# Where two operands of an edge kernel lie: targets' offsets and softmax marks read from PSUM

## The chip, the cores and the metric

The kernel runs on one core of one Trainium2 chip. The metric is the device time of one execution in microseconds; the time before is the median of three runs.

## The reference

A layer of a graph network with 12500 nodes of 128 channels and 400000 edges. The edges come sorted by target (`dst`). Cut to what matters:

```python
h = relu(layernorm(x))
message = (h @ w_src + b_src)[src] + (h @ w_dst)[dst]
rad_w = silu(silu(edge_attr_32 @ fc_w1 + fc_b1) @ fc_w2 + fc_b2) @ fc_w3 + fc_b3
message = message * edge_weight1 * rad_w
message = message @ w_sep + b_sep                    # 8 heads x (16 for scores + 16 values)
alpha = smooth_leaky_relu(message.heads[:, :, :16])
score = einsum("ehk,ahk->eh", alpha, alpha_dot)      # one score per edge and head
att = segment_softmax(score, dst)                    # over the edges of one target
out = segment_sum(value * att, dst) @ w_proj + b_proj
return x + out
```

## The kernel before, in words

**Tiling.** A first stage normalizes the nodes and writes two tables to DRAM, `t_src` and `t_dst` (one row of 128 per node). Then `windows` runs over the edges. A section is 512 edges (`SEC`), four tiles of 128; a step `k` works on two sections, 1024 edges, and there are 391 steps (`NP`). A last stage divides the sums, projects them and adds `x`. A second path, for edges that are not sorted, stands in an Else branch that does not run here.

**The order.** `tc.manual_schedule()` keeps the order in which the program is written, so each engine runs its instructions in the order in which `step` (L1053) calls the helpers. `step(k)` mixes work of several steps: it loads for steps up to `k + 6`, gathers for `k + 2`, does the small network of the edge attributes for `k + 3` to `k`, the message of `k`, the scores of `k - 1`, and the weighted values and sums of step `c = k - 13` (`LAG`), because the softmax of the edges lies between. Semaphores are set between engines wherever a tile is written by one and read by another.

**The gathers.** `gather(k, f)` (L819) issues, from POOL's queue, four indirect DMAs for a section, each of which fetches 128 rows of `t_src` by a column of `idx`, a tile in SBUF. There are three buffers for each of the two sections of a step. TensorE turns the fetched tiles in `sources` (L887, L892).

**Targets' offsets.** Every 16 steps `prep_load` loads sources and targets of 128 tiles as rows, `prep_make` (L746) subtracts from each target the first one of its section, and `prep_turn` (L755) turns both on TensorE, through one PSUM tile "misc", and copies them to SBUF: `idx` for the gathers and `loc` for `one_hot`. `one_hot(c)` (L987) compares `loc` with `lane` (0 to 127 in each partition) on VectorE (L991, 504 results per partition; L994, 8 more for the last place of the window). `sums(c)` (L1012, L1018) multiplies this with the weighted values and accumulates in "misc"; L1022 adds `bare` and leaves the result in `ob`.

**The softmax.** For eight steps (16 sections, 8 heads: 128 partitions of 512 scores) there is one round, `m`. `load_sm` (L942) loads marks from DRAM, one word for each edge that is 0 or a large negative number where a new target begins, with each section's row repeated for its 8 heads. `softmax_up` (L948, L950) and `softmax_down` (L953, L955) are two running maxima with these marks as the first operand; `softmax_exp` (L958) subtracts (L960) and takes Exp on ScalarE; `softmax_T` (L973) turns the result in four transposes through "misc" and copies it. They are called in steps 2, 3 and 4 of each eight, at the end of `step`.

**PSUM.** All eight banks are used: "m1", "misc", "p3" (two), "pa", "V", "pm0" and "pm1". "m1" serves `e_T`, `mlp1` and `scores`; "misc" serves `prep_turn`, `mlp1`, `softmax_T` and `sums`.

**Others that the prediction names.** `split_md` (L806) makes three bf16 parts of a tile in four pieces, two of them on VectorE (L813, L817). `values(c, f)` (L999) makes "V" on TensorE (L1005), and VectorE multiplies it by the weights into `pvx` (L1007). `alphas` (L909) and `alphas_sum` (L917, L919) make `al` from "pa". `radial` is L884, `message` L899 and L906. `add_x` (L1040, L1044) adds a bias to four node tiles in step 7 of each eight, 25 times in all.

Of the kernel before, what the change touches and what calls it, by code (L numbers as in the profile page):

```python
# [56 lines left out]
def gnn_kernel(ctx: ExitStack, tc: tile.TileContext, a: dict, out: bass.AP):  # L57
# [44 lines left out]
    def blocks(t0, t1):  # L102
# [17 lines left out]
                   allow_small_or_imprecise_dtypes=True)  # L120
    zc = 5
# [591 lines left out]
    def windows():  # L713
# [7 lines left out]
        with tc.tile_pool(name="wk2", bufs=2) as sp, tc.tile_pool(name="ps", bufs=1, space=PSUM) as pp, \  # L721
                tc.manual_schedule(), ExitStack() as held:
            lp = held.enter_context(tc.tile_pool(name="ld", bufs=2, side="right"))
            prep, e_g, d_g, w_g, md, gath = {}, {}, {}, {}, {}, {}
            eTs, h1s, h2s, ohT, m3, mr, mTs, als, S_all, sms, Ps, Pem, pvx, ohs, accs, xs, Ms, pms, p3s, rads, made = (
                {} for _ in range(21))
# [19 lines left out]
            def prep_make(u):  # L746
                ri, rb = made[u]
                rows = lp.tile([P, 2, P], F32, name="rows", bufs=1)
                rf = lp.tile([P, 1], F32, name="rf", bufs=1)
                nc.vector.tensor_copy(rf, rb)  # L750
                nc.vector.tensor_copy(rows[:T, 0, :], ri[:T, 0, :])
                nc.vector.tensor_scalar(rows[:, 1, 0:T], ri[:, 1, 0:T], rf, None, op0=ALU.subtract)
                made[u] = rows

            def prep_turn(u):  # L755
                rows = made.pop(u)
                pt = pp.tile([P, 2, P], F32, name="misc")
                nc.tensor.transpose(pt[:, 0, 0:T], rows[:T, 0, :], ident[:T, :T])
                nc.tensor.transpose(pt[:T, 1, :], rows[:, 1, 0:T], ident)
                if u:  # L760
                    idx = lp.tile([P, T], I32, name="idx")
                    nc.vector.tensor_copy(idx, pt[:, 0, 0:T])
                else:
                    idx = idx0
# [54 lines left out]
            def gather(k, f):  # L819
                gs = lp.tile([P, TS, C], F32, name=f"gs{f}", bufs=3)  # L820
                u = k // 16
                idx, _ = prep[u]
# [16 lines left out]
            def mlp1(k):  # L839

                p1 = [pp.tile([P, 2 * T], F32, name=n) for n in ("m1", "misc")]
# [100 lines left out]
            def load_sm(m):  # L942
                sms[m] = sp.tile([P, SEC + 1], BF16, name="sm")
                at = same[0:1, m * MQ * SEC:m * MQ * SEC + 1]
                at = bass.AP(at.tensor, at.offset, [[SEC, MQ], [0, H], [1, SEC + 1]])
                nc.sync.dma_start(out=sms[m], in_=at)

            def softmax_up(m):  # L948
                Ms[m] = sp.tile([P, 2, SEC], F32, name="M")
                nc.vector.tensor_tensor_scan(Ms[m][:, 0, :], sms[m][:, 0:SEC], S_all[m], RESTART,  # L950
# [491 lines left out]
```

## Time and profile before

| | us |
|---|---|
| median of 3 runs | 4320.27 |
| lowest, highest | 4319.8, 4326.04 |
| the profiled execution | 4318.65 |
| its span, first to last instruction | 4316.9 |

The mean granted TensorE clock in the profiled execution is 0.969. The first gather starts 89.2 us after the span's start and the last at 4113.6 us; what follows the last gather is the work of the last 13 steps, the joining of windows and the last stage.

How to read it: PE is TensorE's matmuls, PEld its loads of weights, DVE VectorE, ACT ScalarE, POOL GpSimd, SP the queue from which most DMAs are issued. L12 is line 12 of the kernel. A group's row has the line, engine and operation, the tiles out<-in, the shapes and the count, then the busy time and the mean of one in ns, then the engine's idle time just before and what ended it. A row of the timeline has the start, the duration, both in us, the engine, line and operation, and in brackets the idle time before it and what ended that. A row of windows has the stretch, its length, each engine's busy time with its count, the granted clock as a share, the share of the DMA engines and GB/s. A row of waits has who waited for whom, the total in us, how often and the longest.

### The profile page before, as it was taken

How to read it: one execution, taken by the hardware profiler on the slowest of the kernel's cores; microseconds unless marked ns; L12 is line 12 of the kernel's file. 1: busy time of each engine (PE TensorE's matmuls, PEld its weight loads, DVE VectorE, ACT ScalarE, POOL GpSimd, SP SyncE). 2: the span in 40 equal slices, each digit the busy share in tenths (PEclk: the TensorE clock that was granted, in tenths of full speed). 3: DMA queues.
4: the chain of work that ended last, by engine and by line, in shares of the span. 5: the costliest groups of instructions: out<-in, count | busy, mean ns of one | idle time of the engine just before them, and what ended most of it. 6: DMA issues, size and time to landing. Idle time of an engine off the chain costs nothing. (4 is left out here: it accounts for less than half of the span.)

```text
span 4316.9 us, 86772 instructions
## 1 busy us (share of the span) xinstructions
PE 3929.3 (91%) x29228; PEld 2402.1 (56%) x29228; DVE 3128.6 (72%) x6152; ACT 1919.4 (44%) x4505; POOL 3063.7 (71%) x3148
## 2 busy tenths in 40 slices
PE   6779999999999999999999999999999999999964
PEld 5335555555555555555555555555555555555553
DVE  6457777777777777777777777777777777777764
ACT  6334444444444444444444444444444444444411
POOL 1667777777777777777777777777777777777701
PEclk9889999999999999999999999999999999999987
DMA  5766776776776776776777776767676676676625
GB/s 192 236 191 177 195 191 178 197 189 174 195 190 171 198 189 177 192 191 183 187 188 190 182 185 179 178 186 183 171 187 184 175 187 182 171 187 178 164 60 191
DMA packets 592627, 788.16 MB, mean 183 GB/s; under 512 B 124473, under 2 KB 390814, under 8 KB 592044
## 3 DMA queue, kind: packets, MB, share of 16 engines
q1 hardware_dynamic: 384090, 519.34, 40.4%
q0 software_dynamic: 100416, 205.44, 23.1%
q10 hardware_dynamic: 107666, 57.76, 4.6%
q8 instruction: 232, 3.80, 0.4%
q14 instruction: 223, 1.83, 0.1%
HBM read 642.94 MB, written 139.58 MB: 181 GB/s over the span
## 5 line engine op out<-in xcount | busy, mean ns | idle before, releaser
L825 POOL DMA_INDIRECT gs<-t_src,idx x3125 | 3049.3, 976 | 1063.0 <-issue 783.0
L914 ACT ACTIVATE sl<-pa,c_b_a 128x512 f32<-128x512 f32 x782 | 536.9, 687 | 1123.6 <-PE pa L912 1108.2
L1005 PEld LDWEIGHTS V<-c_w_v,mT 128*128 128x128 f32 x6048 | 749.1, 195 | 315.8 <-DVE ob L1022 132.5
L1005 PE MATMUL V<-c_w_v,mT 128*128 128x128 f32 x6048 | 887.1, 291 | 0.0
L1007 DVE TENSOR_TENSOR pvx<-V,Pem 128x512 f32<-128x512 f32 x756 | 520.7, 689 | 476.7 <-PE V L1005 463.4
L912 PE MATMUL pa<-mT,c_w_a 128*128 128x512 f32 x1564 | 812.6, 602 | 8.0 <-DVE al L919 4.1
L919 DVE SCALAR_TENSOR_TENSOR al<-pa,sl 128x512 f32<-128x512 f32 x782 | 539.7, 690 | 361.1 <-ACT sl L914 356.1
L892 PEld LDWEIGHTS pm<-ident,gs 128*128 128x128 f32 x3125 | 397.7, 141 | 526.5 <-issue 406.8
L884 DVE SCALAR_TENSOR_TENSOR rad<-p,c_fc_b,w_b 128x512 f32<-128x512 f32 x782 | 549.9, 745 | 106.0 <-PE p L876 81.0
L1018 PEld LDWEIGHTS misc<-pvx,oh 128*64 128x64 f32 x6250 | 365.5, 141 | 414.8 <-ACT h L848 409.5
L1018 PE MATMUL misc<-pvx,oh 128*64 128x136 f32 x6250 | 469.3, 294 | 118.2 <-ACT h L848 118.2
L892 PE MATMUL pm<-ident,gs 128*128 128x128 f32 x3125 | 499.7, 277 | 77.7 <-DMA gs<-t_src,idx 73.2
L906 DVE SCALAR_TENSOR_TENSOR mT<-pm,c_b_src,rad 128x512 f32<-128x512 f32 x782 | 550.6, 746 | 25.4 <-PE pm L899 24.5
L862 ACT ACTIVATE h<-p,b 128x512 f32<-128x512 f32 x391 | 288.5, 738 | 435.3 <-PE p L859 369.3
L876 PE MATMUL p<-h,w3b 64*128 64x512 f32 x1564 | 409.4, 601 | 11.1 <-ACT h L862 11.1
L899 PE MATMUL pm<-ohT,m 64*128 64x512 bf16 x2346 | 321.2, 379 | 0.0
L932 ACT ACTIVATE Sp<-m,b_s 128x512 f32<-128x512 f32 x196 | 134.7, 687 | 418.4 <-PE m L929 416.3
L844 PE MATMUL m<-eT,w1b 64*128 64x256 f32 x782 | 276.0, 433 | 1.0 <-ACT eT L837 1.0
L844 PE MATMUL misc<-eT,w1b 64*128 64x256 f32 x782 | 276.0, 433 | 0.0
L859 PE MATMUL p<-h,w2b 64*64 64x256 f32 x3128 | 260.5, 403 | 13.7 <-DVE rad L884 13.7
L991 DVE TENSOR_TENSOR oh<-lane,loc 128x504 f32<-128x504 f32 x391 | 264.4, 676 | 0.0
L848 ACT ACTIVATE h<-misc,b 128x256 f32<-128x256 f32 x391 | 193.2, 494 | 138.4 <-PE misc L844 131.5
(165 smaller groups left out, 3626.3 us busy)
## 6 DMA issues: line engine op xcount, KB each, us to landing
w_b<-in_edge_weight SPq DMA_DIRECT2D x390, 512.0 KB
d_b<-in_dst SPq DMA_DIRECT2D x390, 256.0 KB
sc_d<-Sp SPq DMA_DIRECT2D x196, 256.0 KB
gs<-t_src,idx POOLq DMA_INDIRECT x3125
e_t<-in_edge_attr ACTq DMA_DIRECT2D x390, 128.0 KB
win<-ob SPq DMA_DIRECT2D x391, 68.0 KB
agg<-ob SPq DMA_DIRECT2D x782, 33.5 KB
md<-t_dst SPq DMA_DIRECT2D x782, 32.0 KB
```

The lines of the kernel that those rows point to most:

```text
L825: nc.gpsimd.indirect_dma_start(out=gs[:, t, :], out_offset=None, in_=t_src[:, :], in_offset=bass.IndirectOffsetOnAxis(ap=idx[:, t0 + t:t0 ...
L844: nc.tensor.matmul(p1[q], w1b[s, :], eTs[k][s, :], start=True, stop=True)
L876: nc.tensor.matmul(p3s[k][:, f, 0:SEC], w3b[s, :], h2s[k][s, :], start=True, stop=True)
L884: nc.vector.scalar_tensor_tensor(rad[:, s], p3[:, f, 0:n], b3, w_g[k][:, s], op0=ALU.add, op1=ALU.mult)
L892: nc.tensor.matmul(pms[k, f][:, t * T:(t + 1) * T], gs[:, t, :], ident, start=(t == 0), stop=False, is_transpose=True, skip_group_check=True)
L906: nc.vector.scalar_tensor_tensor(mTs[k][:, s], pms.pop((k, f))[:, 0:n], b_n, rad[:, s], op0=ALU.add, op1=ALU.mult)
L912: nc.tensor.matmul(pa[:, 0:n], w_a, mTs[k][:, f * SEC:f * SEC + n], start=True, stop=True)
L914: nc.scalar.activation(sl[:, 0:n], pa[:, 0:n], AF.Silu, bias=b_a, scale=1.0)
L919: nc.vector.scalar_tensor_tensor(al, pa, 0.25, sl, op0=ALU.mult, op1=ALU.add)
L1005: nc.tensor.matmul(V[:, t, :], mTs[c][:, o:o + T], w_v, start=True, stop=True)
L1007: nc.vector.tensor_mul(pvx[c][:, f, 0:n, 0:C].rearrange("p t (h k) -> p t h k", h=H), V[:, 0:n, :].rearrange("p t (h k) -> p t h k", h=H), ...
L1018: nc.tensor.matmul(acc[f * W:(f + 1) * W, :], ohs[c][:, f * TS + t, :], pvx[c][:, f, t, :], start=(t == 0), stop=(t == n - 1), skip_group_ ...
```

## The change

Five edits.

1. Constants: `spread`, a bf16 matrix of 16 rows and 128 columns that is 1 where column // 8 is the row, made by five VectorE instructions.
2. "misc" becomes one PSUM tile for the whole of `windows`. Its first half (256 words per partition) serves what "misc" served; the second half holds two sets of targets' offsets. `loc_turn` writes them there, `loc` in SBUF and its copy go, and `one_hot` reads them from PSUM. `one_hot` is called behind `sums(c - 1)` instead of ahead of `alphas_sum(k - 1, 0)`. The turn for `u = 0` in step 5 goes; its `idx` is that of the first stage.
3. `softmax_T` is done in two halves of two transposes and one copy each, the first behind `values(c, 1)`, the second where the whole was.
4. The marks are loaded as 16 rows, and `spread_marks` multiplies them by `spread` into a tile "m1", from which the scan reads.
5. `add_x` adds each of the four tiles by itself.

A tile "misc" of the tail is made in the first half, too.

```diff
+    part8 = const.tile([P, 1], F32, name="part8")
+    nc.vector.tensor_scalar(part8, part, float(H), None, op0=ALU.mult)
+    spread = const.tile([MQ, P], BF16, name="spread")
+    below = const.tile([MQ, P], F32, name="below")
+    nc.vector.tensor_scalar(below, lane[:MQ, :], part8[:MQ], None, op0=ALU.subtract)
+    above = const.tile([MQ, P], F32, name="above")
+    nc.vector.tensor_scalar(above, below, 0.0, None, op0=ALU.is_ge)
+    nc.vector.scalar_tensor_tensor(spread, below, float(H), above, op0=ALU.is_lt, op1=ALU.mult)
...
+            bank = pp.tile([P, BANK], F32, name="misc")
+            half = bank[:, 0:BANK // 2]
...
             def prep_make(u):
...
-                nc.vector.tensor_copy(rows[:T, 0, :], ri[:T, 0, :])
-                nc.vector.tensor_scalar(rows[:, 1, 0:T], ri[:, 1, 0:T], rf, None, op0=ALU.subtract)
+                nc.vector.tensor_copy(rows[:T, :], ri[:T, 0, :])
+                rel[u] = sp.tile([P, T], F32, name="rel")
+                nc.vector.tensor_scalar(rel[u], ri[:, 1, 0:T], rf, None, op0=ALU.subtract)
...
             def prep_turn(u):
                 rows = made.pop(u)
-                pt = pp.tile([P, 2, P], F32, name="misc")
-                nc.tensor.transpose(pt[:, 0, 0:T], rows[:T, 0, :], ident[:T, :T])
-                nc.tensor.transpose(pt[:T, 1, :], rows[:, 1, 0:T], ident)
...
-                loc = sp.tile([T, P], F32, name="loc", bufs=3)
-                nc.vector.tensor_copy(loc, pt[:T, 1, :])
-                prep[u] = (idx, loc)
+                pt = half
+                nc.tensor.transpose(pt[:, 0:T], rows[:T, :], ident[:T, :T])
+                idx = lp.tile([P, T], I32, name="idx")
+                nc.vector.tensor_copy(idx, pt[:, 0:T])
+                prep[u] = idx
+
+            def loc_turn(u):
+                o = BANK // 2 + u % 2 * P
+                locs[u] = bank[:T, o:o + P]
+                nc.tensor.transpose(locs[u], rel.pop(u), ident)
...
             def load_sm(m):
-                sms[m] = sp.tile([P, SEC + 1], BF16, name="sm")
+                sms[m] = sp.tile([MQ, SEC + 1], BF16, name="sm")
                 at = same[0:1, m * MQ * SEC:m * MQ * SEC + 1]
-                at = bass.AP(at.tensor, at.offset, [[SEC, MQ], [0, H], [1, SEC + 1]])
-                nc.sync.dma_start(out=sms[m], in_=at)
+                nc.sync.dma_start(out=sms[m], in_=bass.AP(at.tensor, at.offset, [[SEC, MQ], [1, SEC + 1]]))
+
+            def spread_marks(m, o):
+                pt = pp.tile([P, SEC], F32, name="m1")
+                nc.tensor.matmul(pt, spread, sms[m][:, o:o + SEC], start=True, stop=True)
+                return pt
 
             def softmax_up(m):
                 Ms[m] = sp.tile([P, 2, SEC], F32, name="M")
-                nc.vector.tensor_tensor_scan(Ms[m][:, 0, :], sms[m][:, 0:SEC], S_all[m], RESTART,
+                nc.vector.tensor_tensor_scan(Ms[m][:, 0, :], spread_marks(m, 0), S_all[m], RESTART,
                                              op0=ALU.add, op1=ALU.max)
 
             def softmax_down(m):
                 M = Ms[m]
-                nc.vector.tensor_tensor_scan(M[:, 1, ::-1], sms[m][:, SEC:0:-1], M[:, 0, ::-1], RESTART,
+                nc.vector.tensor_tensor_scan(M[:, 1, ::-1], spread_marks(m, 1)[:, ::-1], M[:, 0, ::-1], RESTART,
                                              op0=ALU.add, op1=ALU.max)
...
-            def softmax_T(m):
-                pt = pp.tile([T, TS, P], F32, name="misc")
-                for t in range(TS):
-                    nc.tensor.transpose(pt[:, t, :], Ps[m][:, t * T:(t + 1) * T], ident)
-                Pem[m] = sp.tile([T, TS, MQ, H], F32, name="Pem")
-                nc.scalar.copy(Pem[m].rearrange("p t q h -> p t (q h)"), pt)
+            def softmax_T(m, i):
+                pt = half[:T, :].rearrange("p (t q) -> p t q", t=TS // 2)
+                t0 = i * (TS // 2)
+                for t in range(TS // 2):
+                    nc.tensor.transpose(pt[:, t, :], Ps[m][:, (t0 + t) * T:(t0 + t + 1) * T], ident)
+                if i == 0:
+                    Pem[m] = sp.tile([T, TS, MQ, H], F32, name="Pem")
+                nc.scalar.copy(Pem[m][:, t0:t0 + TS // 2].rearrange("p t q h -> p t (q h)"), pt)
...
             def one_hot(c):
-                _, loc = prep[c // 16]
+                loc = locs[c // 16]
...
                     u = t[:n, t0 - quads[i][0]:t1 - quads[i][0], :]
-                    nc.vector.tensor_tensor(u, u, b_out[:n].unsqueeze(1).to_broadcast([n, t1 - t0, C]), op=ALU.add)
+                    for j in range(t1 - t0):
+                        nc.vector.tensor_add(u[:, j, :], u[:, j, :], b_out[:n])
...
-                if k == 5:
-                    prep_turn(0)
...
+                if k % 16 == LAG - 1 and has(k - LAG + 1):
+                    loc_turn(k // 16)
...
-                if has(c):
-                    one_hot(c)
...
                 if has(c - 1):
                     sums(c - 1)
+                if has(c):
+                    one_hot(c)
...
                 if has(c):
                     values(c, 1)
+                if has(k - MP) and r == 4:
+                    softmax_T(m - 1, 0)
...
                 if has(k - MP) and r == 4:
-                    softmax_T(m - 1)
+                    softmax_T(m - 1, 1)
```

More of the change, by code (lines that the diff above doesn't have):

```diff
@@ L821, in gather @@
                 u = k // 16
-                idx, _ = prep[u]
+                idx = prep[u]
                 t0 = (k % 16 * 2 + f) * TS
@@ L839, in mlp1 @@
             def mlp1(k):
-                p1 = [pp.tile([P, 2 * T], F32, name=n) for n in ("m1", "misc")]
+                p1 = [pp.tile([P, 2 * T], F32, name="m1"), half[:, 0:2 * T]]
                 for q in range(2):
@@ L1012, in sums @@
             def sums(c):
-                acc = pp.tile([P, ROW], F32, name="misc")
+                acc = half[:, 0:ROW]
                 for t in range(TS):
```

15 lines of the change are left out of this document (5 added, 10 removed).

## The prediction

> **What bounds the kernel now.** I read the page first, then the gathers' own line, then the waits, then the timeline of single steps.
>
> ```profile
> span 4316.9 us, 86772 instructions
> ...
> PE 3929.3 (91%) x29228; PEld 2402.1 (56%) x29228; DVE 3128.6 (72%) x6152; ACT 1919.4 (44%) x4505; POOL 3063.7 (71%) x3148
> ...
> L825 POOL DMA_INDIRECT gs<-t_src,idx x3125 | 3049.3, 976 | 1063.0 <-issue 783.0
> ...
> L991 DVE TENSOR_TENSOR oh<-lane,loc 128x504 f32<-128x504 f32 x391 | 264.4, 676 | 0.0
> ```
>
> PE looks like the bound and POOL, at 71%, does not. But POOL's idle time is "issue", which is no wait for anybody: it comes between every two gathers. One line's view of L825, and a window from the end of start-up to the last gather, say more:
>
> ```profile
> L825 POOL DMA_INDIRECT gs<-t_src,idx x3125: 938/944/2658, 89.2 to 4113.6; - x196
> ...
> 131.00:4114.00 3983.00, 3023.32 (x3101) 0.98 0.70 184
> ```
>
> In 3983 us stand 3101 gathers, one every 1.284 us. A gather has a median of 0.944 us. What is left between two, (3983 - 3023.3)/3101, is 0.31 us; the 0.30 stands in front of every gather of the timeline below, so a gather without trouble costs 1.249 us (0.944 + 0.305), and 3101 of them 3873 us. POOL is thus full all the time. The 110 us above 3873 are 96 us of gathers that took longer than the median (3023.3 - 3101 x 0.944) and 14 us of pauses. And PE waits for gathers:
>
> ```profile
> PEld pm L892 <- DMA gs<-t_src,idx: 117.6, 168, 3.7
> ...
> PE pm L892 <- DMA gs<-t_src,idx: 73.2, 81, 3.5
> ```
>
> Two steps of the timeline show why some are long:
>
> ```profile
> 1134.75 1.16 PE L1005 MATMUL V<-c_w_v,mT 128*128 128x128 f32 x8
> ...
> 1135.59 1.22 DVE L950 TENSOR_TENSOR_SCAN M<-sm,S 128x512 f32<-128x512 bf16 x1
> ...
> 1136.14 1.41 POOL L825 DMA_INDIRECT gs<-t_src,idx  x1 [0.30 <-issue]
> ...
> 1137.50 0.68 DVE L991 TENSOR_TENSOR oh<-lane,loc 128x504 f32<-128x504 f32 x1
> ...
> 1137.86 1.14 POOL L825 DMA_INDIRECT gs<-t_src,idx  x1 [0.30 <-PE misc L844]
> ...
> 1139.17 1.40 DVE L884 SCALAR_TENSOR_TENSOR rad<-p,c_fc_b,w_b 128x512 f32<-128x512 f32 x2
> 1139.30 0.95 POOL L825 DMA_INDIRECT gs<-t_src,idx  x1 [0.30 <-issue]
> ...
> 1144.65 1.16 PE L1005 MATMUL V<-c_w_v,mT 128*128 128x128 f32 x8
> ...
> 1145.49 1.22 DVE L955 TENSOR_TENSOR_SCAN M<-sm,M 128x512 f32<-128x512 bf16 x1
> ...
> 1145.54 1.91 POOL L825 DMA_INDIRECT gs<-t_src,idx  x1 [0.30 <-issue]
> ...
> 1147.46 0.63 ACT L962 ACTIVATE Pr<-M 128x512 f32<-128x512 f32 x1 [0.64 <-DVE M L960]
> ...
> 1148.54 1.28 ACT L914 ACT_TABLE_LOAD   x1
> ...
> 1151.15 1.65 PEld L1018 LDWEIGHTS misc<-pvx,oh 128*64 128x64 f32 x16 [3.38 <-ACT h L848]
> ...
> 1158.22 1.06 PE L1005 MATMUL V<-c_w_v,mT 128*128 128x128 f32 x8
> ```
>
> A gather that starts while a DVE instruction with both tensors in SBUF runs ends late, by that instruction's end less 0.13 us of its own start: L991 ends at 1138.18, 0.32 into the gather, which takes 0.944 + 0.19 = 1.14. Both scans do it too (1.41 and 1.91). L884, with one tensor in PSUM, covers a gather that takes 0.95. So the loop is paced by POOL, and POOL is held by DVE's reads.
>
> PE is close behind. Its own need for a round of eight steps:
>
> ```profile
> 2027.28 1.16 PE L1005 MATMUL V<-c_w_v,mT 128*128 128x128 f32 x8
> ...
> 2036.18 1.16 PE L1005 MATMUL V<-c_w_v,mT 128*128 128x128 f32 x8
> ```
>
> ```profile
> 1076.50:1158.30 81.80, 79.25 (x601) 48.20 (x600) 62.73 (x119) 38.25 (x91) 62.45 (x64) 0.98 0.72 192
> 1151.15:1154.56 3.41, 3.41 (x23) 3.05 (x24) 2.10 (x5) 0.32 (x1) 2.50 (x4) 0.51 0.63 64
> ```
>
> A step (from the first V to the next step's) is 8.90 us without scores (2027.28 to 2036.18) and 9.90 with (1134.75 to 1144.65). Step 4 of each eight takes 13.57 (1144.65 to 1158.22): Exp waits for the scans on DVE, a table load of 1.28 us follows, and PE stands still for 3.38 us at L1018 until ACT is through; then the granted clock is 0.51 for 3.41 us, in the windows' second row. The need is 4 x 8.90 + 4 x 9.90 + (13.57 - 8.90) = 79.9 us. POOL's for the round's 64 gathers is 64 x 1.249 = 79.9 as well, and the round in the windows' first row took 81.80. The 1.9 us between are the delayed gathers.
>
> **The change part by part.** These rows carry the prices:
>
> ```profile
> L950 DVE TENSOR_TENSOR_SCAN M<-sm,S 128x512 f32<-128x512 bf16 x49 | 59.5, 1214 | 29.6 <-DMA S<-sc_d 29.6
> L955 DVE TENSOR_TENSOR_SCAN M<-sm,M 128x512 f32<-128x512 bf16 x49 | 59.5, 1214 | 0.0
> L960 DVE TENSOR_TENSOR M<-S,M 128x512 f32<-128x512 f32 x49 | 33.9, 692 | 1.7
> ...
> L1044 DVE TENSOR_TENSOR xs<-xs,c_b_proj 128x512 f32<-128x512 f32 x24 | 16.4, 684 | 0.0
> ...
> L813 DVE TENSOR_TENSOR mr<-md,m 128x128 f32<-128x128 f32 x391 | 110.9, 284 | 57.2 <-ACT m L810 56.9
> ...
> L817 DVE TENSOR_TENSOR m<-mr,m 128x128 bf16<-128x128 f32 x391 | 111.8, 286 | 0.0
> ...
> L899 PE MATMUL pm<-ohT,m 64*128 64x512 bf16 x2343 | 321.2, 379 | 0.0
> ```
>
> *Delays removed and left.* If a gather's start falls anywhere in its 1.249 us, an instruction of length d delays one with the chance (d - 0.13)/1.249, by (d - 0.13)/2 in the mean. That gives 391 x 0.119 = 47 us for L991, 98 x 0.47 = 46 for the scans, 24 x 0.12 = 3 for L1044, 49 x 0.126 = 6 for L960 and 782 x 0.0097 = 8 for L813 and L817. The sum is 110 against the 96 measured, so I scale by 0.88. The change gives L991 and both scans one operand from PSUM, and cuts L1044 into four short pieces (of some 0.28 us, as L813; 96 x 0.0097 = 1). L960, L813 and L817 keep both in SBUF. Removed: (47 + 46 + 2) x 0.88 = 83 us; left: 13. POOL's round is then 79.9 + 13/48.5 (3101 gathers are 48.5 rounds) = 80.2.
>
> [...]
>
> *one_hot moved behind the sums.* Its 0.68 us and the small instruction after it (under 0.2) leave the place ahead of al(0) and stand between ob and pvx of the step's second half:
>
> ```profile
> 2011.20 1.16 PE L1005 MATMUL V<-c_w_v,mT 128*128 128x128 f32 x8
> 2011.57 0.29 DVE L1022 TENSOR_TENSOR ob<-misc,bare 128x136 f32<-128x136 f32 x1
> ...
> 2012.39 0.69 DVE L1007 TENSOR_TENSOR pvx<-V,Pem 128x512 f32<-128x512 f32 x1 [0.54 <-PE V L1005]
> ...
> 2014.04 0.69 DVE L919 SCALAR_TENSOR_TENSOR al<-pa,sl 128x512 f32<-128x512 f32 x1 [0.75 <-ACT sl L914]
> ...
> 2015.15 1.16 PE L1005 MATMUL V<-c_w_v,mT 128*128 128x128 f32 x8
> ```
>
> DVE idles 0.54 + 0.75 = 1.29 us there, so 0.87 fits before al starts at 2014.04. Queued behind it on DVE are pvx, L817 and al; who waits first is PE's next V, which needs pvx's bank: pvx ends at 2012.71 + 0.69 = 2013.40, and V starts at 2015.15. Price 0; without that cover, 391 x 0.87 = 340 us. From PSUM L991 may take from 0.67 (the 0.69 of L1007, one operand in PSUM, for eight more elements) to 0.70 (L884's 1.40 for two); I take 0.68. [...]
>
> *Marks spread by PE.* 98 matmuls of 512 bf16 columns: 0.14 us each if they flow as L899 (321.2/2343), 0.38 as its mean of one; those run as pairs of halves, so I take 2 x 0.137 = 0.27. One stands at the end of step 2, on PE's path: 0.27 a round. The other stands ahead of step 4's stall of 3.38 us, which covers it (else 0.27 more). Each scan holds bank m1 until it ends; mlp1 of the next step wants it. L955 ends at 1146.71, 2.06 us after its step's V; mlp1 stands behind V (1.16) and pa (1.02) at least, 2.18. Cover 0.1 and the 0.27 just added; as a bound, a scan longer by 0.4 us would cost nothing, one of twice its length 2 x 0.85 a round. The load is 16 rows in place of 128, with the same count on SP: 0.
>
> *softmax_T in halves.* Four transposes as before, but the first two now wait for one_hot (whole bank "misc"). By the rows above, ob ends at 2011.86, one_hot at 2012.73, V at 2012.36: between 0 and 0.37 us of PE a round; at the halved clock of step 4 V ends later and it is 0. I take 0.2. Behind it wait pa and ACT's next sl. ACT makes two copies of half the size, one more fixed part, while it idles after sl.
>
> *The rest at nothing.* prep_turn has one transpose instead of two and loc_turn the other; 25 copies on DVE and u = 0's turn go; four L1044 pieces cost DVE some 0.45 us in one step of eight, under the V that pvx waits for (11 us if uncovered). The constants are five small instructions of DVE at the start, at most 1 us.
>
> *Sum.* PE's round becomes 79.9 + 0.27 + 0.2 = 80.4, or 1.7 less where the clock isn't halved (3.41 us at 0.51). POOL's is 80.2. With both so near they will not always meet; I take 80.55. Against 81.80 that is 1.25 us a round, 48.5 rounds: 60 us. The profiled execution lasted 4318.65 us, with its span of 4316.9; so 4259, and as it lies 1.6 under the median of 4320.27, the forecast is 4260.
>
> **The rivals.**
>
> *All of POOL's time comes out.* If the clock is halved less often, PE's round is 78.7 and POOL alone sets the pace: 83 us less, 4237. For it: steps where PE isn't late are 8.90 and 9.90 throughout. Against: the stall of step 4 stays as it is.
>
> *The reads that are left take the gathers.* PE follows the gathers, so DVE keeps its phase to POOL; L813 or L817 could hit a gather in nearly every step, as the scans do in both rows above. One such instruction can delay by 0.155 us (0.285 - 0.13) at most: 391 x 0.15 = 59, less the 7 counted for both. 4260 + 35 with half of that beyond PE's slack: 4295. Against: the 96 us hold little room for L813 and L817 now.
>
> *PE takes over (slower).* Place: step 4's bank "misc", where the first half of softmax_T waits for one_hot, one_hot for ob, ob for sums, which has just waited 3.38 us. A stall longer by 0.4 us may halve the clock for a second 3.41 us, costing 1.7, while spread (0.27 twice) no longer hides: 79.9 + 0.4 + 1.7 + 0.54 = 82.5 a round, 0.7 over now: +36 us, 4356. It decides once PE's additions pass 81.8 - 79.9 = 1.9 us a round. Against: the rows give 0.5.
>
> *Nothing happens.* Gathers are late for another reason that goes with the same DVE times, such as the SBUF writes, which stay: POOL keeps its 81.8, PE's additions vanish in it, 4320. [...] Against: L884 writes SBUF just as long and delays nobody.
>
> **How the numbers follow.** Forecast (4245 to 4280) 0.60; all of POOL's time 0.14; the reads left 0.12; PE slower 0.08; nothing 0.06. Range 4228 to 4312: its upper end takes in the reads that are left with a hit in every step (4260 + 52 = 4312), its lower end a little beyond POOL's floor; outside are slower, nothing and a part of the second case, 0.19. About 0.2%, 8.6 us, is what a measurement of this kernel can tell from no change. Faster: 0.60 + 0.14 + most of 0.12 = 0.84; same: 0.06 + 0.02 = 0.08; slower 0.08.
>
> **What would show it.** Right: the gathers' mean falls from 976 to about 948 with the median at 944; gathers under L991 and the scans take 0.94; gathers under L960, L813 and L817 are still late; steps without scores stay at 8.90; pvx of the second half starts some 0.3 us later and no V waits for it; PE's waits for gathers fall from 191 us to under 100. Wrong: long gathers under L991's successor; PE idle ahead of softmax_T's first half, spread or mlp1; step 4 over 13.6 us, or more stretches at half clock; a scan much over 1.214 us.

## The result and the profile after

The changed kernel takes 4246.64 us in the median of four runs (4244.78 to 4253.0), the kernel before beside it 4321.68: a ratio of 0.9828 [0.9811, 0.9845], 75 us less. The forecast was 4260. The profiled execution of the changed kernel lasted 4246.18 us, with a mean granted clock of 0.973.

On two more chips of the experiments the kernel before takes 4324 and 4325 us, and variants of the change gain there as it does here. On four others the kernel before itself takes some 5300 us; the changed kernel ran on one of them and was slower by 2% there. These have a section of their own; what stands ahead of it on times is about chips with 4320.

The page of the changed kernel: span, engines, and the groups that are the gathers (L825 before) and one_hot (L991 before), with busy time and mean.

```profile
span 4244.4 us, 87582 instructions
...
PE 3923.8 (92%) x29325; PEld 2397.9 (56%) x29325; DVE 3118.1 (73%) x6203; ACT 1917.4 (45%) x4554; POOL 2987.0 (70%) x3148
...
L835 POOL DMA_INDIRECT gs<-t_src,idx x3125 | 2972.6, 951 | 1066.2 <-issue 769.3
...
L1007 DVE TENSOR_TENSOR oh<-lane,misc 128x504 f32<-128x504 f32 x391 | 262.3, 671 | 0.0
```

The gathers' mean fell from 976 to 951 ns, 77 us over 3125 of them; one_hot takes as long from PSUM as it did from SBUF (671 ns against 676). The windows from the end of start-up to the last gather, then one round of eight steps, then 3.41 us in step 4 of two neighbouring rounds (the granted clock is the third number from the end):

```profile
131.00:4041.00 3910.00, 3734.83 (x27946) 2236.55 (x27947) 2927.73 (x5735) 1807.82 (x4301) 2947.38 (x3101) 0.99 0.69 187
1071.59:1150.86 79.27, 76.54 (x584) 46.06 (x584) 60.61 (x120) 37.26 (x90) 60.06 (x63) 1.00 0.72 190
1145.80:1149.21 3.41, 2.91 (x20) 2.16 (x18) 2.39 (x7) 0.73 (x2) 2.73 (x3) 1.00 0.71 211
1225.30:1228.71 3.41, 3.41 (x12) 2.60 (x13) 2.33 (x6) 0.37 (x1) 2.73 (x3) 0.50 0.85 193
```

The same 3101 gathers that stood in 3983 us now stand in 3910: 73 of the 75 us. POOL is still full: behind 285 us from the span's start, no gap between two gathers is over 0.32 us. Of the 37 us above 3873 (3101 x 1.249), late gathers are 20 (2947.4 - 3101 x 0.944) and pauses 17; before they were 96 and 14.

Steps 2 to 4 of one round in the timeline, the counterpart of the steps shown before:

```profile
1128.32 1.16 PE L1021 MATMUL V<-c_w_v,mT 128*128 128x128 f32 x8
...
1128.85 1.21 DVE L964 TENSOR_TENSOR_SCAN M<-m,S 128x512 f32<-128x512 f32 x1
1129.19 0.94 POOL L835 DMA_INDIRECT gs<-t_src,idx  x1 [0.30 <-issue]
...
1133.85 0.67 DVE L1007 TENSOR_TENSOR oh<-lane,misc 128x504 f32<-128x504 f32 x1
1134.18 0.94 POOL L835 DMA_INDIRECT gs<-t_src,idx  x1 [0.30 <-issue]
...
1138.23 0.39 PE L959 MATMUL m<-sm,spread 16*128 16x512 bf16 x1
1138.54 1.16 PE L1021 MATMUL V<-c_w_v,mT 128*128 128x128 f32 x8
1139.06 1.22 DVE L969 TENSOR_TENSOR_SCAN M<-m,M 128x512 f32<-128x512 f32 x1
1139.17 0.95 POOL L835 DMA_INDIRECT gs<-t_src,idx  x1 [0.30 <-issue]
1140.31 0.69 DVE L974 TENSOR_TENSOR M<-S,M 128x512 f32<-128x512 f32 x1
1140.43 1.39 POOL L835 DMA_INDIRECT gs<-t_src,idx  x1 [0.30 <-issue]
...
1144.72 0.89 PEld L1034 LDWEIGHTS misc<-pvx,oh 128*64 128x64 f32 x16 [3.06 <-ACT h L858]
...
1147.45 0.20 PEld L991 LDWEIGHTS misc<-ident,Pr 128*128 128x128 f32 x2 [0.69 <-DVE oh L1010]
1147.46 0.44 PE L991 MATMUL misc<-ident,Pr 128*128 128x128 f32 x2 [0.50 <-DVE oh L1010]
...
1150.86 0.97 PEld L1021 LDWEIGHTS V<-c_w_v,mT 128*128 128x128 f32 x8
```

Gathers that start under a scan (1129.19, 1139.17) or under one_hot (1134.18) now take 0.94 or 0.95 us. The one that starts 0.12 us into S - M (L974, L960 before), which still has both tensors in SBUF, takes 1.39. Step 4 goes from 1138.54 to 1150.86: 12.32 us, against 13.57. Its stall at the sums is 3.06 us in place of 3.38, as the spread matmul now fills a part of that time, and its clock was not halved. Against that stands the new wait of 0.50 us for one_hot.

The waits of the changed kernel: who waited for whom, us in total, how often, the longest.

```profile
PE misc L991 <- DVE oh L1010: 18.4, 30, 3.8
PE m L854 <- DVE M L964: 18.1, 1, 18.1
PE pm L902 <- DMA gs<-t_src,idx: 10.4, 11, 2.9
...
PEld pm L902 <- DMA gs<-t_src,idx: 40.4, 111, 3.2
```

PE's waits for gathers fell from 117.6 + 73.2 to 40.4 + 10.4 us.

### The profile page after: what moved, and what is told of

Its sections match the earlier page's. It is cut to its first block, busy times and chain, and to the rows that moved or that the text cites. A ratio compares the mean times of both kernels' runs of the same rounds, so it can differ in the third digit from the quotient of the medians.

```text
span 4244.4 us, 87582 instructions
## 1 busy us (share of the span) xinstructions
PE 3923.8 (92%) x29325; PEld 2397.9 (56%) x29325; DVE 3118.1 (73%) x6203; ACT 1917.4 (45%) x4554; POOL 2987.0 (70%) x3148
## 3 DMA queue, kind: packets, MB, share of 16 engines
q1 hardware_dynamic: 378602, 513.71, 40.4%
## 5 line engine op out<-in xcount | busy, mean ns | idle before, releaser
L835 POOL DMA_INDIRECT gs<-t_src,idx x3125 | 2972.6, 951 | 1066.2 <-issue 769.3
L929 DVE SCALAR_TENSOR_TENSOR al<-pa,sl 128x512 f32<-128x512 f32 x782 | 540.5, 691 | 605.3 <-ACT sl L924 595.5
L1034 PEld LDWEIGHTS misc<-pvx,oh 128*64 128x64 f32 x6250 | 355.2, 138 | 396.0 <-ACT h L858 388.2
L1034 PE MATMUL misc<-pvx,oh 128*64 128x136 f32 x6250 | 456.4, 289 | 104.1 <-ACT h L858 103.8
L902 PE MATMUL pm<-ident,gs 128*128 128x128 f32 x3125 | 476.0, 274 | 10.7 <-DMA gs<-t_src,idx 10.4
L886 PE MATMUL p<-h,w3b 64*128 64x512 f32 x1564 | 403.3, 593 | 5.5 <-ACT h L872 5.4
L854 PE MATMUL m<-eT,w1b 64*128 64x256 f32 x782 | 274.6, 432 | 19.2 <-DVE M L964 18.1
L869 PE MATMUL p<-h,w2b 64*64 64x256 f32 x3128 | 261.1, 404 | 14.4 <-DVE rad L894 14.4
L1007 DVE TENSOR_TENSOR oh<-lane,misc 128x504 f32<-128x504 f32 x391 | 262.3, 671 | 0.0
L922 PEld LDWEIGHTS pa<-mT,c_w_a 128*128 128x128 f32 x1564 | 241.6, 195 | 20.0 <-DVE mT L916 7.6
```

What stands on the lines that cost most here:

```text
L835: nc.gpsimd.indirect_dma_start(out=gs[:, t, :], out_offset=None, in_=t_src[:, :], in_offset=bass.IndirectOffsetOnAxis(ap=idx[:, t0 + t:t0 ...
L854: nc.tensor.matmul(p1[q], w1b[s, :], eTs[k][s, :], start=True, stop=True)
L886: nc.tensor.matmul(p3s[k][:, f, 0:SEC], w3b[s, :], h2s[k][s, :], start=True, stop=True)
L902: nc.tensor.matmul(pms[k, f][:, t * T:(t + 1) * T], gs[:, t, :], ident, start=(t == 0), stop=False, is_transpose=True, skip_group_check=True)
L922: nc.tensor.matmul(pa[:, 0:n], w_a, mTs[k][:, f * SEC:f * SEC + n], start=True, stop=True)
L929: nc.vector.scalar_tensor_tensor(al, pa, 0.25, sl, op0=ALU.mult, op1=ALU.add)
```

## The experiments on chips with 4320 us

**The marks from SBUF again.** All of the change but the marks, which are 128 rows in SBUF with no spread matmul.

```diff
-    sms[m] = sp.tile([MQ, SEC + 1], BF16, name="sm")
-    nc.sync.dma_start(out=sms[m], in_=bass.AP(at.tensor, at.offset, [[SEC, MQ], [1, SEC + 1]]))
+    sms[m] = sp.tile([P, SEC + 1], BF16, name="sm")
+    at = bass.AP(at.tensor, at.offset, [[SEC, MQ], [0, H], [1, SEC + 1]])
+    nc.sync.dma_start(out=sms[m], in_=at)
-    spread_marks(m, 0), S_all[m]
+    sms[m][:, 0:SEC], S_all[m]
-    spread_marks(m, 1)[:, ::-1]
+    sms[m][:, SEC:0:-1]
```

> The marks loaded as 128 rows into SBUF again, scans read both tensors from SBUF; the rest as changed. Where the kernel before takes 4320 us. Theory (gathers pace the loop, the scans delay them): the scans' delays of some 50 us come back on POOL, PE's two spread matmuls and its 18 us of waits for m1 go; gathers' mean 966 to 970 ns; 4265 to 4300 us, so 0.987 to 0.995 of before. Rival (PE paces, and the delays vanish in its slack): 0.978 to 0.983, at or below the changed kernel's ratio, since two matmuls and the m1 wait are gone.

Measured: 4260.07 us, 0.9854 [0.9834, 0.9875] of the kernel before. The intervals of this ratio and of the changed kernel's overlap, so the 13 us between them are not secured by the times alone. Its groups:

```profile
L835 POOL DMA_INDIRECT gs<-t_src,idx x3125 | 2988.0, 956 | 1064.8 <-issue 795.8 <-DVE sm L343 87.1 <-DMA gs<-t_src,idx 50.7
...
L970 DVE TENSOR_TENSOR_SCAN M<-sm,M 128x512 f32<-128x512 bf16 x49 | 59.6, 1216 | 0.0
```

The gathers are busy 15.4 us longer than in the changed kernel (2988.0 - 2972.6), about what the time shows. The direction is the theory's and the size is not, with a time 5 us under its range and a mean of 956 ns against 966 to 970: 50 us of delays by the scans were to come back, and 19.5 came (the second table below). In this kernel a scan caught 43 gathers; before the change the two scans caught 83. So in this kernel fewer gathers start under a scan; all 43 that did were late. S - M, which delayed gathers by 9.3 us in the changed kernel, met none here.

Not all of the 15.4 us is delay, though. What late gathers lose (those over 0.960 us, their time above 0.944) is 31.9 us here, 23.4 in the changed kernel and 99.9 before: 8.5 us between the first two. The other 7 us are the ordinary gathers, with a mean of 946.1 ns in this execution and 943.7 in the changed kernel's. That goes with the execution and not with the kernel: two executions of this same kernel on other chips have 945.9 and 943.2. So of the 76 us of late gathers that the change removes, some 8 are the marks', net of what S - M takes, and some 68 those of the offsets, one_hot's place and add_x.

**The first transposes of softmax_T later.** The changed kernel with its first half moved behind `pa` and the message transposes.

```diff
-    if has(k - MP) and r == 4:
-        softmax_T(m - 1, 0)
     if has(k - 1):
         sl = alphas(k - 1, 1)
     if has(k):
         sources(k, 1)
+    if has(k - MP) and r == 4:
+        softmax_T(m - 1, 0)
```

> The changed kernel, with the first half of softmax_T put behind pa and the message transposes of its step in place of right behind V, so that one_hot has 1.6 us more to end. Where the kernel before takes 4320 (gathers pace): PE's wait for one_hot (14.5 us in all) goes and half-clock stretches may fall below 17: theory 4225 to 4246 us; rival (POOL paces alone): 4244 to 4248. Where the kernel before takes some 5300 us: there step 4 of each eight took 16.4 us in the changed kernel and 13.2 with one_hot moved alone, nearly all of the change's loss. Theory (the first half's wait for one_hot, behind a late ob, lets PE stand still and halves the clock): step 4 falls below 14.5 us and the time to 0.99 to 1.005 of before. Rival (two transposes groups with two copies on ACT cost it, wherever they stand): step 4 stays above 15.5 us and the ratio at 1.01 to 1.02.

Measured: 4244.96 us, 0.9814 [0.9798, 0.9831], not to be told from the changed kernel. The page's row of the gathers and the waits:

```profile
L835 POOL DMA_INDIRECT gs<-t_src,idx x3125 | 2971.2, 951 | 1066.1 <-issue 799.7
```

```profile
PE pm L902 <- DMA gs<-t_src,idx: 23.3, 35, 2.4
```

Of PE's 18.4 us of waits for one_hot at the transposes one is left, of 3.8 us, behind the last gather; PE waits 12.9 us longer for gathers instead (23.3 against 10.4). The rival holds: POOL paces, and PE's waits lie in its slack.

**The times follow the gathers.** With these two there are four kernels whose time can be set against the busy time of the gathers, each from its own row:

```
kernel                      median us   gathers busy us   difference
before                        4321.68            3049.3       1272.4
marks from SBUF               4260.07            2988.0       1272.1
changed                       4246.64            2972.6       1274.0
changed, transposes later     4244.96            2971.2       1273.8
```

The times differ by 77 us, the differences by 2 (by 5, when the profiled execution's own time stands in place of the median). What the loop costs is what its gathers cost, with PE's work, waits and clock differing between the four. The gaps say the same: in none of the four is one between two gathers over 0.40 us once the first 280 us are past.

## Which instructions hold a gather

For every kernel each gather's time above 0.944 us (where it is over 0.016) was put to the DVE instruction that was running some 0.05 us after the gather's start. Sums in us, with the number of gathers in brackets; "ohT" is L869 before and L879 after, a comparison of one int32 tensor in SBUF with a constant of each partition; "split" is L813 and L817.

```
kernel                    one_hot     scans       S - M      ohT         split      add_x
before                    37.2 (216)  50.3 (83)    0.0 (0)    0.3 (2)    3.4 (39)   4.6 (17)
changed                    0.0 (0)     0.0 (0)     9.3 (26)   6.0 (61)   3.5 (55)   0.3 (7)
marks from SBUF            0.0 (0)    19.5 (43)    0.0 (0)    4.8 (48)   3.8 (64)   0.7 (5)
transposes later           0.0 (1)     0.0 (0)     5.0 (18)   7.3 (55)   5.3 (80)   0.5 (5)
on chips with 5300 us
order alone               41.1 (140)  39.3 (68)    0.0 (0)   13.8 (139)  1.0 (20)   2.5 (10)
changed                    0.0 (0)     0.0 (0)    15.6 (43)  16.0 (165)  1.5 (28)   1.5 (14)
marks from SBUF            0.0 (0)    56.5 (89)    0.0 (0)   10.5 (109)  1.4 (24)   1.1 (11)
marks from SBUF, again     0.0 (0)    66.0 (93)    0.0 (0)   14.1 (138)  1.7 (29)   1.0 (9)
offsets from SBUF         41.3 (117)   0.0 (0)     8.5 (32)  14.2 (148)  0.6 (10)   1.6 (13)
offsets from SBUF, 2nd    46.8 (124)   0.0 (0)     5.4 (28)  17.0 (159)  1.0 (15)   1.5 (13)
offsets from SBUF, 3rd    40.7 (109)   0.0 (0)     9.1 (33)  15.0 (152)  1.4 (23)   1.5 (13)
changed, both loads        0.0 (0)     0.0 (0)    15.2 (44)  13.4 (149)  0.9 (15)   1.3 (12)
down scan in PSUM          0.0 (0)     0.0 (0)     0.0 (0)   16.0 (153)  1.4 (29)   0.8 (7)
```

one_hot delays gathers wherever its offsets come from SBUF, ahead of the sums or behind them, and none (one, in one kernel) where they come from PSUM. The scans do the same with their marks. S - M delays gathers as long as both its tensors lie in SBUF, but in the five of these kernels with a 0 no gather met it. Other causes of late gathers stayed under 5 us together in each kernel.

A 0 can mean that an instruction holds nobody or that no gather met it. So here are the gathers that start under an instruction with at least 0.2 us of it left:

```
                             both tensors in SBUF            one in PSUM
                             gathers   late   mean ns        gathers   late   mean ns
one_hot, before | changed        154    153      1162            119      0       944
scans, before | changed           83     83      1550             90      0       943
S - M, changed | down scan
  in PSUM (chips with 5300)       43     43      1308             40      0       947
```

Gathers still start under these instructions as before or nearly so, and take their ordinary time. It is also the gather's start that counts: before the change one_hot starts 0.17 to 0.80 us into 219 gathers and runs on past 0.87, and none of them is late.

These counts are durations of single gathers and hold on both kinds of chip; the times of the second group need the next section. The runs behind its rows:

*Order alone*: the kernel before with one_hot behind the sums.

```diff
-    if has(c):
-        one_hot(c)
     if has(k - 1):
         alphas_sum(k - 1, 0, *sl)
...
         sums(c - 1)
+    if has(c):
+        one_hot(c)
```

> The kernel before with nothing but one_hot called behind the sums. Theory: both tensors still in SBUF, the gathers stay late, 4321 +- 15. Rival (the new place gave the gain): 4260 to 4285, with the gathers' mean still about 976.

Measured: 5302.18 us, 0.997 [0.9946, 0.9995].

```profile
L825 POOL DMA_INDIRECT gs<-t_src,idx x3125 | 3056.8, 978 | 1987.0 <-issue 749.8 <-PE m L835 375.8 <-PE p L876 258.5
```

The gathers' mean is 978 ns, as before the change (976). Moving one_hot alone frees POOL of nothing: 41.1 us under it against 37.2.

*Offsets from SBUF*: the changed kernel with the turned offsets copied to SBUF.

```diff
-    locs[u] = bank[:T, o:o + P]
-    nc.tensor.transpose(locs[u], rel.pop(u), ident)
+    pt = bank[:T, o:o + P]
+    nc.tensor.transpose(pt, rel.pop(u), ident)
+    locs[u] = sp.tile([T, P], F32, name="loc", bufs=3)
+    nc.vector.tensor_copy(locs[u], pt)
```

> The changed kernel with the targets' offsets copied from PSUM to SBUF once in 16 steps, so that one_hot, at its new place behind the sums, reads both tensors from SBUF. Theory: 391 x 0.105 = 41 us of delays come back (20 to 70, as its phase to the gathers falls out), time about 4285 (4265 to 4310), the late gathers are those under one_hot. Rival (the new place gave the gain, not the operand): time 4245 to 4250.

> The offsets copied from PSUM to SBUF once per sixteen steps and compared from there; one_hot stays behind the sums. Theory: one_hot's 391 instructions delay gathers again where their phase falls on them, 37 us before the change, perhaps more as DVE's order is another; gathers' mean 961 to 968 ns; 4270 to 4295 us. Rival (one_hot's place behind the sums is what keeps gathers clear of it, not the operand's memory): gathers' mean 951 as in the changed kernel and 4246 us.

> The offsets copied from PSUM to SBUF once per sixteen steps and compared from there; one_hot stays behind the sums, the marks stay spread. Where the kernel before takes 4320 us. Theory (gathers pace the loop, one_hot delays them): one_hot's delays come back, 37 us before the change, more or less as its phase to the gathers falls behind the sums; gathers' mean 957 to 968 ns; 4260 to 4290 us, so 0.986 to 0.993 of before. Rival (one_hot's place behind the sums, not its operand, is what freed the gathers): gathers' mean 951 and 0.980 to 0.984, as the changed kernel.

Measured: 1.0166 [1.0123, 1.021], 1.0231 [1.0166, 1.0296] and 1.0157 [1.0109, 1.0204], all on chips with 5300 us, so none of the expected times was put to the test. What the groups of the third run say of the mechanism is the theory's number:

```profile
L837 POOL DMA_INDIRECT gs<-t_src,idx x3125 | 3018.4, 966 | 2134.4 <-issue 746.5 <-PE m L847 527.8 <-PE p L888 290.2
...
L1009 DVE TENSOR_TENSOR oh<-lane,loc 128x504 f32<-128x504 f32 x391 | 263.6, 674 | 0.2
```

The mean is 966 ns, with one_hot's 41 us in it; the rival's was 951, and the changed kernel's on such a chip is 956.

*Marks from SBUF* on those chips, the edit of above:

> The changed kernel with the marks loaded as 128 rows again and both scans reading them from SBUF; the offsets stay in PSUM. Theory (a gather is held by a DVE instruction with both tensors in SBUF): gathers under the scans are late again by some 0.4 to 0.6 us each, 98 x 0.4 to 0.5 = 40 to 50 us more of POOL, the gathers' mean 951 -> about 965, time about 4285 (4275 to 4295). Rival (TensorE's spreading and the wait for bank m1 are a price on the path and the scans are harmless): the 0.6 us a round go, time 4220 to 4247.

> The marks loaded as 128 rows into SBUF again, scans read both tensors from SBUF; the rest as changed. Theory: 98 scans delay gathers again, by 50 us of POOL before the change; the spread matmuls and PE's 18 us of waits for m1 go, which PE's round of 80 us hides only in part. Gathers' mean 966 to 970 ns; 4260 to 4290 us. Rival (the gain is the order of one_hot, or PE's work, not the reads): 4246 or less, since two matmuls and the m1 wait are gone.

Measured: 1.0085 [1.0057, 1.0112] and 1.0144 [1.009, 1.0198]; gathers' mean 969 ns in the first. There the scans' delays came back in full (56.5 and 66.0 us).

*Both loads*: the changed kernel, which also loads the marks as 128 rows into a tile that nobody reads.

```diff
+    more = sp.tile([P, SEC + 1], BF16, name="more")
+    at = bass.AP(at.tensor, at.offset, [[SEC, MQ], [0, H], [1, SEC + 1]])
+    nc.sync.dma_start(out=more, in_=at)
```

> The changed kernel with, in addition, the old load of the marks as 128 rows into a tile that nobody reads: the DMA's price alone. Theory: 4246 +- 5. Rival (the 112 rows saved in each of 49 loads gave a part of the gain): 4260 to 4285.

Measured: 1.0114 [1.0081, 1.0148], gathers' mean 954 ns, 956 in the changed kernel on another such chip. So no delay of gathers by that load was seen; what it costs in time was not seen on a chip with 4320 us.

*Down scan in PSUM*: the changed kernel, whose downward scan writes over its marks in PSUM, so that S - M reads one tensor from there.

```diff
-    nc.vector.tensor_tensor_scan(M[:, 1, ::-1], spread_marks(m, 1)[:, ::-1], M[:, 0, ::-1], RESTART,
+    tops[m] = pt = spread_marks(m, 1)
+    nc.vector.tensor_tensor_scan(pt[:, ::-1], pt[:, ::-1], M[:, 0, ::-1], RESTART,
...
-    nc.vector.tensor_sub(M[:, 0, :], S_all[m], M[:, 1, :])
+    nc.vector.tensor_sub(M[:, 0, :], S_all[m], pt)
+    nc.vector.tensor_copy(M[:, 1, 0:SEC:SEC - 1], pt[:, 0:SEC:SEC - 1])
```

> The changed kernel, and the downward scan writes into the marks' own PSUM tile, from which S - M reads its second operand; the two end columns are copied to SBUF. Theory: S - M has no longer both tensors in SBUF, so its 26 late gathers (9.4 us in all) go; gathers' mean 948; the marks' bank is held some 0.7 us longer in one step of eight, so PE's wait for m1 grows from 0.37 to about 1 us in that round: 4240 to 4275 us, with the gathers' mean as the test. Rival (S - M's delays have another cause): mean stays 951.

Measured: 1.0219 [1.0157, 1.0281], gathers' mean 953 ns against 956 for the changed kernel beside it. (Late gathers lose 22.7 us against 38.8; the mean falls by less, since the ordinary gathers take 945.8 ns in this execution against 943.1.) S - M's 43 late gathers went to none, while its own mean is 687 ns against 692 in the changed kernel:

```profile
L976 DVE TENSOR_TENSOR M<-S,m 128x512 f32<-128x512 f32 x49 | 33.7, 687 | 1.7
```

By the table of times this would be worth up to 9 us on a chip with 4320; it was not tried there.

## The chips on which the change is slower

Beside each of these runs the kernel before took 5297 to 5319 us. The changed kernel itself, as a control:

> The changed kernel itself, as a control beside the parts taken back in the runs that follow. Theory (gathers pace the loop and the two edits free them of delays): 4240 to 4255 us on a chip whose kernel before takes 4320, gathers' mean 951. If the kernel before takes some 5300 us, as it did beside the first four runs, with gathers no longer back to back: then the delays cost little, and the changed kernel should be between 0.99 and 1.015 of before, where the parts taken back stood.

Measured: 5413.88 us, 1.0199 [1.0142, 1.0256]. So the gathers' delays are gone here too and the time is 2% above before, more than was expected. Its page:

```profile
span 5403.0 us, 87582 instructions
...
PE 4244.7 (79%) x29325; PEld 2547.0 (47%) x29325; DVE 3112.4 (58%) x6203; ACT 1910.2 (35%) x4554; POOL 3000.8 (56%) x3148
...
L835 POOL DMA_INDIRECT gs<-t_src,idx x3125 | 2986.4, 956 | 2189.3 <-issue 733.3
```

POOL works 3001 us out of 5403 and stands idle ahead of gathers for 2189 us, 1123 more than on the other chip: it is not full and does not pace. A stretch of the timeline shows what holds everybody:

```profile
2011.30 1.15 PE L1034 MATMUL misc<-pvx,oh 128*64 128x136 f32 x16
...
2013.37 1.02 PE L922 MATMUL pa<-mT,c_w_a 128*128 128x512 f32 x2
...
2013.66 1.41 DVE L894 SCALAR_TENSOR_TENSOR rad<-p,c_fc_b,w_b 128x512 f32<-128x512 f32 x2 [2.54 <-PE V L1021]
...
2018.05 0.30 DVE L1038 TENSOR_TENSOR ob<-misc,bare 128x136 f32<-128x136 f32 x1 [2.98 <-issue]
...
2018.19 0.69 ACT L924 ACTIVATE sl<-pa,c_b_a 128x512 f32<-128x512 f32 x1 [6.57 <-PE pm L909]
...
2018.50 0.94 POOL L835 DMA_INDIRECT gs<-t_src,idx  x1 [2.21 <-PE pm L909]
```

sl needs pa, which ended at 2014.39, and ob needs the sums, which ended at 2012.45; both start at 2018, with the gather, within half a microsecond of each other. The trace's semaphore records say why: PE's updates stop at 2013.64 and ten of them come between 2017.97 and 2018.38, though matmuls that give one had ended from 2014.39 on (the ends of matmuls are modelled in these records, their starts are not). Counted between 250 and 3900 us, stretches of over 1.5 us without an update of PE, in which at least four matmuls that give one had ended 0.1 us or more before the next update: none in the kernel before, the changed kernel, the marks from SBUF and the later transposes on chips with 4320; 235 to 257 of them, together 758 to 836 us, in each of the nine runs with all gathers on the other chips.

The change's own loss lies in step 4. Mean length of the steps of a round in us, from the starts of L886 (L876 before), steps 50 to 380:

```
step of eight                     0      1      2      3      4      5      6      7
before, 4320                   9.79   9.94   9.79  10.49  12.96   9.92   8.92  10.10
changed, 4320                  8.92   9.90   9.52  10.29  12.63   9.90   8.90   9.93
order alone, 5300             12.46  13.00  13.42  11.76  13.23  12.58  11.80  12.97
changed, 5300                 11.91  13.19  12.89  12.27  16.43  12.05  11.75  13.47
marks from SBUF, 5300         12.04  13.30  12.62  12.81  16.19  12.05  11.48  13.53
```

Where the kernel before takes 5300 us, the other steps differ by up to 1.2 us in either direction, but step 4 is 3.2 us longer with the changed kernel than with the order alone (on two different chips), and nearly as long without the spread matmuls. That points to the first half of softmax_T. The changed kernel's waits on such a chip agree:

```profile
PE misc L991 <- DVE oh L1010: 89.8, 45, 3.8
```

That is 71 us more than on the other chip. It is the place named for the rival in which PE takes over. The three kernels with offsets from SBUF bear this out only in part: there the transposes wait for ob in place of one_hot, 52 to 61 us, and step 4 takes 14.8 to 15.2 us, yet they are as slow (1.0157 to 1.0231), with longer steps 0 (12.4 to 12.7) and 2 (13.9 to 14.2). The run with later transposes, made to test it, came on a chip with 4320 us; that this place costs the 2% was therefore not shown.

**A quarter of the gathers left out.** The last run asked who paces, with the kernel before.

```diff
-    for t in range(tiles(k, f)):
+    for t in range(min(3, tiles(k, f))):
         nc.gpsimd.indirect_dma_start(
...
-    pms[k, f][:, t * T:(t + 1) * T], gs[:, t, :], ident,
+    pms[k, f][:, t * T:(t + 1) * T], gs[:, min(t, 2), :], ident,
```

> The kernel before with three of each section's four gathers; the fourth tile is taken from the third again, so the fetch of every fourth tile of source rows is left out. PE, DVE and ACT do the same work, POOL a quarter less. Theory (before the change POOL paced the loop at 81.8 us for a round of eight steps, PE's own need being 79.9 or less): POOL falls to some 62 us a round and PE sets the pace; 4190 to 4240 us, 0.970 to 0.982 of before, with hardly a wait of PE for gathers. Rival (PE paces, the gathers only follow): 0.995 to 1.0.

Measured: 4478.61 us, 0.8419 [0.8387, 0.845] of a kernel before of 5312.16. Both expectations were for a loop that POOL or PE fills, and neither foresaw this. The engines' row of its page:

```profile
PE 3949.5 (88%) x29228; PEld 2413.6 (54%) x29228; DVE 3120.9 (70%) x6152; ACT 1909.0 (43%) x4505; POOL 2319.7 (52%) x2367
```

Stretches without PE's updates are 76 here, 259 us, and PE's work is the same 29228 matmuls. So on this chip the late semaphores go with the gathers, or with something that the gathers bring about (their transfers, the pace itself). Which of them, and why two kinds of chip differ, stays open.

## Why the prediction was right

*POOL paces, and late gathers are the loss.* Right, and shown by the table of times, 2 us of scatter over 77 us of difference, and by the gathers' row, which has no gaps to fill.

*Instructions with both tensors in SBUF hold a gather to their end.* Right for one_hot, scans, S - M and add_x. The delay is the time from 0.13 us behind the gather's start to the instruction's end; this comes out to within 0.01 us for most of the gathers under one_hot, and the scans let go 0.06 us earlier. With at least 0.2 us of one_hot left at their start, 153 of 154 gathers are late; of 219 that one_hot meets behind their first 0.17 us none is. The gathers take their row numbers from `idx` in SBUF. Which part of a gather is held, the reading of `idx` or another, no run shows. The list was too short: ohT, with a single tensor in SBUF, delayed 61 gathers by 6.0 us.

*Removed 83, left 13.* The windows give 96 - 20 = 76 removed and 20 left. one_hot, scans and add_x lost 91.8 us by the table; S - M and ohT took 15 back, as in the gather at 1140.43 above, which the scan no longer holds and which meets S - M. S - M was put at 6 x 0.88 and ohT at nothing.

*PE's round of 80.4, both together 80.55.* This is the term that was mis-sized. The gathers of steps 50 to 380 took 81.93 us for each 64 before the change and take 80.32 after it, close to the 80.2 that the working had for POOL alone. PE ran the same steps in 80.00 us a round (the row of steps above): it catches up 13 us on POOL's gathers in them. So PE needs no more than 80.00, and the 0.35 us that 80.55 has over POOL's 80.2 was not lost. (81.93 - 80.32) x 48.5 is 78 us; with 3 us of longer pauses it is the 75 measured, in place of 1.25 x 48.5 = 60.

The working had charged the halved clock's 1.7 us to PE in every round. Between 250 and 4000 us the trace has 17 stretches at half clock in 47 rounds; before the change it has 30. With 17/47 of 1.7 PE needs an estimated 80.4 - 1.7 + 0.6 = 79.3, under POOL's 80.2, and the working's own terms would then have given POOL's round: (81.80 - 80.2) x 48.5 = 78 us, 4242. The marks-from-SBUF kernel has 31 such stretches again and still takes what its gathers take. That the forecast came within 15 us is in part luck: the delays removed were overrated (83 for 76), which hid a part of what the bound by PE, which was not there, took off the gain.

*one_hot behind the sums costs nothing.* Right as far as it was tested: no wait of V for pvx is among the longer ones, and the order alone gave 0.997, though on a chip with 5300 us.

*Spread 0.27 a round, the second one covered, m1 free in time.* A spread takes 0.39 us, step 2 has a median of 9.22 us against 8.90 in the kernel with marks from SBUF, so 0.32; the second one shortened the stall of step 4 by about as much (medians of 3.38 before and 3.05 after, 3.32 without the spread matmuls). The cover of m1 held in every round but the first, which nothing in the working looked at: there the scan waits for the load of S, m1 stays taken, and PE waits once for 18.1 us. Before, PE stood still for 11.9 us at that time (L929), and POOL's pauses grew by 3 us.

*softmax_T's first half 0.2 a round.* It was 0.50 in 27 rounds, 18.4 us in 30 waits. Taking it away changed no time. ACT's two copies take 364 ns each (L994), the one of twice the size took 569 (L978).

*Scans and one_hot from PSUM as fast as from SBUF.* Right: 1214 and 671 ns against 1214 and 676.

*The rivals.* "All of POOL's time comes out", 4237, and the forecast, 4260, stand on either side of 4246.6: its condition, the clock halved less often, came true. The reads that are left did not take the gathers: L823 and L827 have 3.5 us. "Nothing happens" fell. "PE takes over" did not come on chips with 4320; on the others something at its place did, with the cause open. That a stall longer by 0.4 us may halve the clock for a second 3.41 us was the author's guess: the one stretch of 6.83 us before the change between 250 and 4000 us (from 2461.53) stands at a wait of PE of 2.55 us at L1018, and of waits as long one has a stretch of 3.41 us (1150.9) and one has none (1561.4).

## What to carry to other kernels

POOL's queue, one gather after another with the same 0.3 us between, was full at 70% busy on a chip with 4320 us. With such a queue, set its group's busy time against the time over several versions before believing the busier engine. Where it issues gathers, look which VectorE instructions are running when gathers start; give each long one that reads two tensors from SBUF an operand from PSUM (under one_hot 153 of 154 gathers were late without it, none of 119 with it), longest and most frequent first, and look which of the short ones move into the gap. The gain of 2% where POOL paces (0.9828) was a loss of 2% on a chip where it does not (1.0199), so see a change on more than one chip.

## What the runs showed that was not expected

- A comparison with one int32 tensor in SBUF and a constant of each partition (128 x 512, bf16 result, 498 ns) holds gathers as those with two tensors do: 61 in the changed kernel, 6.0 us, 109 to 165 on the other chips. Unlike one_hot it also holds a gather near its end: 38 gathers of the changed kernel (1.6 us in all) in which it started 0.37 to 0.45 us after the gather and ended 0.85 to 0.93 us after the gather's start; they end 0.12 us behind it.
- Gathers that nothing holds average 943.1 to 943.8 ns in nine of the executions and 945.3 to 946.1 in five, and one kernel fell into both groups. Over 3125 gathers that is 7 us, as much as one of the effects looked for here.
- The kernel before took 4320 to 4325 us on some chips and 5297 to 5319 on others, with 235 to 257 stretches of some 3 us there, in kernels with all gathers, in which PE's semaphore updates came late; a quarter fewer gathers left 76 of these and took 16% off the time.
